# Row maxima of attention scores by a relu and an add-max, in an attention-and-scan kernel

## The chip, the core and the metric

The kernel runs on one core of a Trainium2 chip. The metric is the device time of one launch in microseconds (us). The core has a matrix engine (TensorE, PE in the views; its weight loads are PEld), a vector engine (VectorE, DVE), an activation engine (ScalarE, ACT), GpSimd (POOL) and SyncE (SP), which issues the DMAs. Each engine runs its own queue in order and waits on semaphores for the others.

## The reference

For 16 images of 256 channels by 32 x 32 pixels (1024 tokens) two residual layers are computed in f32. Only the first layer's attention is touched here:

```
tok  = gn(x) + pos
qkv  = layernorm(tok) @ w_qkv                  # 4 heads of 32
dots = einsum('bihd,bjhd->bhij', q, k) * 32**-0.5
attn = softmax(dots, axis=-1)                  # 1024 x 1024 per head
out  = einsum('bhij,bjhd->bihd', attn, v)
tok  = out @ w_out + b_out + tok               # then a feed-forward part
```

The second layer is a state-space model: convolutions and projections, then a scan over the 1024 tokens, h = dA * h + (d_t * u_t) * B_t, for 512 channels x 64 states, an output y = sum of h * C_t, a gate and a projection.

The softmax subtracts the largest score of each row. The kernel needs these row maxima before it can compute exp(dots - max).

## The kernel before, in words

**The scan sets the pace.** For every image there are 256 scan units (`UNITS`), each of 128 partitions x 1024 tokens. A unit is a DMA of one broadcast row block (`load`, tile `dub`), a multiplication on GpSimd (`inputs`, L905), a matmul with 48 rows for the decay (`decay`, L914) and its exp on ScalarE (L916), both in a two-bank PSUM tile `a` with two buffers, and `tensor_tensor_scan` on VectorE (`scan`, L922). After eight units the 64 states are summed on TensorE (`outputs`, L947 and L959, tile `yb`), with copies out by ScalarE (L953, L963).

**All other work is fitted in between.** The layers around the scan are Python generators. Image b+1's attention and scan inputs, and image b-1's gate, run beside image b's scan: the main loop (from L1000) calls, per unit, in this order: load, inputs, the next pieces of `outputs`, scan of unit n, decay of unit n+2, and then one piece of the side work, up to its next `yield`. At the end of the build every compute engine's instructions are tied to the order in which they were written (L1048 to L1058), so that each queue holds exactly this interleaving. Only the first image's attention runs with no scan beside it.

**PSUM has eight banks.** Four belong to the decays (`aps`), one to `yb`, one to accumulations (`accp`), and two to everything else (`mm`). `psum()` takes from `mm` while the scan runs; before the scan it also takes the banks of `aps` in turn.

**The maxima stage** (L411 to L448 of `attention_layer`). `q4` and `k4` hold the queries and keys of the four heads, 32 partitions each, 1024 tokens wide. The loop has 32 steps: 16 chunks of 64 queries (c) x 2 halves of 512 keys (hf). A step begins with `maxima()`, which lets VectorE reduce the two tiles that the step before wrote (L416, tensor_reduce max, PSUM 128x512 to one column of `mx`). Then two PSUM tiles are taken, one for each pair of heads g, and four matmuls (L435), one per head, fill them: 64 queries of each head on 64 partitions, 512 keys wide. Each step also issues one of the DMAs that bring the heads into the layout of the next stage (`to_space`). Then it yields, and the main loop goes on with a scan unit. After the loop the two halves are joined and negated by one more reduce (L445), and TensorE turns the result (L447) for use as a further row of the queries.

After that come the values, the scores again in the other orientation with exp on ScalarE (L503, L511), and the rest of the layer. The tiles of L511 come from the pool `ptp` (tag "pt", four buffers).

Of the kernel before, what the change touches and what calls it, by code (L numbers as in the profile page):

```python
# [11 lines left out]
F32 = mybir.dt.float32  # L12
BF16 = mybir.dt.bfloat16
AF = mybir.ActivationFunctionType
ALU = mybir.AluOpType
AX = mybir.AxisListType
# [3 lines left out]
P = 128  # L20
# [3 lines left out]
HL = 512  # L24
NG = 16
HEADS, DH = 4, 32
INNER = HEADS * DH
NJ = L // P
# [22 lines left out]
def attention_then_scan_kernel(  # L51
# [18 lines left out]
    nc = tc.nc  # L70
    B = x.shape[0]

    def pool(name, bufs, **kw):
        return ctx.enter_context(tc.tile_pool(name=name, bufs=bufs, **kw))
# [5 lines left out]
    ptp = pool("ptp", 4)  # L80
    small = pool("small", 2)
# [14 lines left out]
    def bank(src, name):  # L96
        return src.tile([P, HL], F32, name=name, tag="mm" if src is mm else "av")

    def free_bank(name):
        if spare:  # L100
            return spare.pop()
        if next(alone) is mm:
            return bank(mm, name)
        both = aps.tile([P, L], F32, name=name, tag="a")
        spare.append(both[:, hs(1)])
        return both[:, hs(0)]

    def psum(name, dims=P):
        return (bank(mm, name) if beside["scan"] else free_bank(name))[:dims]
# [7 lines left out]
    def work(name, n=L):  # L117
        return wide.tile([P, L + 2 + CONV], F32, name=name, tag="wide")[:, :n]

    def hwork(name):  # L120
        return half.tile([P, HL], F32, name=name, tag="half")

    def hs(h):
        return ts(h, HL)
# [37 lines left out]
    for k in range(ND):  # L162
# [4 lines left out]
        for j in range(2):  # L167
# [3 lines left out]
                start=(j == 0), stop=(j == 1),  # L171
# [32 lines left out]
    t = work("ones_s")[:1]  # L204
# [3 lines left out]
    for k in range(KC):  # L208
        t = work("rel_s").rearrange("p (i j) -> p i j", j=32)
# [156 lines left out]
    def attention_layer(b):  # L366
# [23 lines left out]
        q4, k4 = work("q4"), work("k4")  # L390
# [17 lines left out]

        mx = small.tile([P, 2, 2 * NJ, 2], F32, name="mx", tag="mx")  # L411
        waiting = []

        def maxima():
            for s, g, c, hf in waiting:
                nc.vector.tensor_reduce(mx[:, g, c, hf : hf + 1], s, AX.X, ALU.max)  # L416
            waiting.clear()

        def against(pair, e):
# [3 lines left out]
        to_space = [  # L423
            partial(spaced, to, src, pair)
            for pair in range(HEADS // 2) for to, src in ((qas, q4), (kas, k4))
        ] + [partial(against, pair, e) for pair in range(HEADS // 2) for e in range(2)]
        for c in range(2 * NJ):
            for hf in range(2):
                maxima()
                for g in range(2):  # L430
                    waiting.append((psum("s_ps"), g, c, hf))
                for h in range(HEADS):
                    g, e = divmod(h, 2)
                    r = ts(h, DH)
                    nc.tensor.matmul(  # L435
                        waiting[g][0][ts(e, 64)], q4[r, ts(c, 64)], k4[r, hs(hf)],
                        start=True, stop=True,
                    )
                if to_space:
                    to_space.pop(0)()  # L440
                yield 1
        maxima()
        del q4, k4, to_space
        neg = small.tile([P, HEADS * NJ], F32, name="neg", tag="neg")
        nc.vector.tensor_reduce(neg, mx.rearrange("p g c k -> p (g c) k"), AX.X, ALU.max, negate=True)  # L445
        ps = psum("neg_ps", HEADS * NJ)[:, :P]
        nc.tensor.matmul(ps, neg, ident, start=True, stop=True)  # L447
        yield 1  # L448
# [2 lines left out]
        for h in range(HEADS):  # L451
            pair, e = divmod(h, 2)
# [6 lines left out]
        for g in range(2):  # L459
            t = work("vv").rearrange("p (j h e) -> p j h e", j=NJ // 2, h=HEADS)  # L460
            nc.vector.memset(t[:, :, :, DH:], 1.0)
            ps = psum("v_ps").rearrange("p (j e) -> p j e", j=NJ // 2)
            for j in range(NJ // 2):
                for k in range(KC):
                    nc.tensor.matmul(
                        ps[:, j, :], xn[k][:, ts(g * (NJ // 2) + j, P)], wv_s[:, k, :],
                        start=(k == 0), stop=(k == KC - 1),
# [14 lines left out]
        for pair in range(HEADS // 2):  # L482
# [3 lines left out]
            for hf in range(2):  # L486
# [11 lines left out]
                for j in range(NJ):  # L498
                    scores = []
                    for e in range(2):  # L500
                        r = ds(2 * DH * e, DH + 1)
                        s = psum("st_ps")
# [6 lines left out]
                    for s in scores:  # L509
                        pt = ptp.tile([P, HL], F32, name="pt", tag="pt")  # L510
# [35 lines left out]
        for hf in range(2):  # L546
            nc.vector.tensor_tensor(ao[:, hs(hf)], ao[:, hs(hf)], sums[:, hs(hf)], ALU.mult)
            for k in range(KC):
                for i, ps in outs:
                    if i == k:  # L550
                        t = tok[k][:, hs(0)]
# [7 lines left out]
        for k, ps in outs:  # L559
            t = tok[k][:, hs(1)]  # L560
# [22 lines left out]
        for hf in range(3):  # L583
            for k, ps in enumerate(outs):
                t = xs[k][:, hs(hf - 1)]
# [386 lines left out]
    def prepare(b):  # L972
        return chain(first_norm(b), attention_layer(b), scan_inputs(b))
# [26 lines left out]
    for n, (b, k, q, e, i) in enumerate(units):  # L1000
        at = n % UNITS
        if at == 0:
            parts = [prepare(b + 1)] if b + 1 < B else []
            total = steps * len(parts)
            if b > 0:
                parts = [first_norm(b + 1), gate_and_store(b - 1), attention_layer(b + 1), scan_inputs(b + 1)]
                if b + 1 == B:
                    parts = parts[1:2]
                total = total + GATE
            side = chain(*parts)  # L1010
            rate, due = rate_for(total, UNITS - AHEAD - 3), 0.0
# [102 lines left out]
```

## Time and profile before

| | |
|---|---|
| median of 3 runs | 13106.57 us (13067.61 to 13129.75) |
| profiled execution, its own time | 13096.86 us |
| its span, first to last instruction | 13095.1 us |
| mean granted TensorE clock | 0.800 |
| L922 scan, VectorE | 4096 x 2278 ns, 9215.1 us |
| L905 multiplication, GpSimd | 4096 x 2417 ns, 9810.6 us |
| L916 exp of the decay, ScalarE | 4096 x 1090 ns, 4462.8 us |
| L416 reduces of the maxima, VectorE | 1023 x 681 ns, 649.0 us in this row |
| L435 matmuls of the maxima, TensorE | 4092 records, mean 619 ns as the row has it |

The page of a profile gives each engine's busy time and its share of the span, then groups of instructions: line, engine, operation, output <- input by the program's names, shapes, count; then busy time, mean length of one in ns, and the idle time of the engine just ahead of them with what ended it. The timeline view gives start and length in us and merges neighbours of one group ("x2"). An f32 matmul appears as two records, each with its own weight load. Records of one engine may overlap a little, as each counts its way through the pipeline. An idle time in square brackets is that of the engine before the instruction. A windows view gives the busy time of each engine in a stretch.

### The profile page before, as it was taken

To read this page: it belongs to the slowest core of one execution; us is meant where nothing else is said; L and a number is where in the kernel's file an instruction comes from. 1 tells how busy PE (TensorE), PEld (TensorE's weight loads), DVE (VectorE), ACT (ScalarE), POOL (GpSimd) and SP (SyncE) were. 2 spreads that over 40 slices of the span, in tenths; PEclk is the share of its full clock that TensorE was granted. 3 is DMA by queue.
4 is the path that set the end of the run, shared out by engine and by line. 5 is a ranking of instruction groups with operands and counts; after the bars stand their busy time and mean duration, and the time that the engine had idled before them with its cause. 6 is when DMAs were issued, how large, how long until landed. Compare 5 with 4: busy or idle time off the path is not lost.

```text
span 13095.1 us, 424083 instructions
## 1 busy us (share of the span) xinstructions
PE 9717.3 (74%) x186800; PEld 5456.0 (42%) x186800; DVE 11666.7 (89%) x7560; ACT 7520.3 (57%) x10421; POOL 9815.4 (75%) x4105
## 2 busy tenths in 40 slices
PE   6676876868778687786868767687686877868767
PEld 2344443444444344443444434444344444444445
DVE  3789999899999899988999898999989899889998
ACT  2465664655646556565665656566465664655654
POOL 0487876878778787786877768787687877878798
PEclk8887977879788697887879878797787977869755
DMA  1467666676666767666666666766667666676676
GB/s 52 165 220 238 208 218 218 220 243 201 221 216 219 235 200 233 216 220 231 211 224 218 213 223 213 236 210 219 218 218 234 205 218 217 218 236 204 227 248 231
DMA packets 1038401, 2820.10 MB, mean 215 GB/s; under 512 B 290370, under 2 KB 368451, under 8 KB 1036548
## 3 DMA queue, kind: packets, MB, share of 16 engines
q1 hardware_dynamic: 1036548, 2792.97, 64.6%
q8 instruction: 1459, 23.90, 0.7%
q14 instruction: 394, 3.23, 0.1%
HBM read 2513.82 MB, written 261.62 MB: 212 GB/s over the span
## 4 chain that ended last, share of the span: by engine, by line
DVE 36%; PE 31%; issue 13%; ACT 11%; DMA 6%; POOL 2%; SPq 1%; DVEq 0%; POOLq 0%; ACTq 0%
DVE h L922 25%; PE yb L947 6%; ACT a L916 5%; DVE mx L416 5%; PE a L914 5%; PE av L491 3%; PE g_ps L688 2%; DMA dub<-dus 2%; PE st_ps L503 2%; POOL dub L905 2%; PE z_ps L639 2%; PE yb L959 1%; PE m_ps L859 1%; PE qk_ps L403 1%; DVE u L674 1%
## 5 line engine op out<-in xcount | busy, mean ns | idle before, releaser
L905 POOL TENSOR_TENSOR dub<-dub,bt 128x1024 f32<-128x1024 f32 x4096 | 9810.6, 2417 | 3229.8 <-DMA dub<-dus 2896.6
L922 DVE TENSOR_TENSOR_SCAN h<-a,dub 128x1024 f32<-128x1024 f32 x4096 | 9215.1, 2278 | 752.0 <-ACT a L916 401.8
L916 ACT ACTIVATE a<-a,acol 128x1024 f32<-128x1024 f32 x4096 | 4462.8, 1090 | 3253.4 <-PE a L914 3206.7
L914 PE MATMUL a<-pieces,pick 48*128 48x512 bf16 x8192 | 1902.6, 455 | 2518.2 <-DVE h L922 2401.8
L947 PEld LDWEIGHTS yb<-h,cd 128*32 128x32 f32 x131072 | 2488.2, 128 | 2781.3 <-issue 1265.6
L947 PE MATMUL yb<-h,cd 128*32 128x64 f32 x131072 | 3255.8, 252 | 476.8 <-ACT y L953 325.2
L914 PEld LDWEIGHTS <-pick 48*128 48x128 bf16 x8192 | 603.3, 95 | 2915.4 <-issue 2467.5
L953 ACT COPY y<-yb 128x256 f32<-128x256 f32 x2048 | 763.6, 373 | 914.7 <-PE yb L947 907.5
L435 PE MATMUL s_ps<-k,q 32*64 32x512 f32 x4092 | 825.7, 619 | 95.5 <-DVE mx L416 95.0
L416 DVE TENSOR_REDUCE mx<-s_ps 128x1 f32<-128x512 f32 x1023 | 649.0, 681 | 15.5 <-PE s_ps L435 15.5
L491 PE MATMUL av<-pt,vv 128*64 128x512 f32 x2048 | 596.1, 662 | 3.0 <-ACT sums L480 1.7
L959 PE MATMUL yb<-turn,y 128*32 128x16 f32 x32768 | 591.4, 214 | 5.8 <-issue 4.9
L511 ACT ACTIVATE pt<-st_ps 128x512 f32<-128x512 f32 x1024 | 554.1, 599 | 60.9 <-PE st_ps L503 59.9
L959 PEld LDWEIGHTS yb<-turn,y 128*32 128x32 f32 x32768 | 573.8, 159 | 6.6 <-issue 5.2
L503 PE MATMUL st_ps<-sp 33*128 33x512 f32 x2048 | 561.8, 622 | 4.5 <-ACT pt L511 3.3
L963 ACT COPY yo<-yb 128x128 f32<-128x128 f32 x512 | 136.1, 266 | 587.8 <-PE yb L959 560.5
L688 PE MATMUL g_ps<-w,xp 128*128 128x256 f32 x1464 | 451.9, 447 | 0.0
L688 PEld LDWEIGHTS g_ps<-w,xp 128*128 128x128 f32 x1464 | 367.3, 326 | 65.5 <-issue 54.0
L435 PEld LDWEIGHTS s_ps<-k,q 32*64 32x64 f32 x4092 | 193.6, 131 | 440.8 <-DVE mx L416 421.1
L859 PE MATMUL m_ps<-w,xs 128*128 128x256 f32 x1024 | 317.5, 460 | 10.4 <-DVE xs L834 10.4
L674 DVE SCALAR_TENSOR_TENSOR u<-up,cwh,u 128x1024 f32<-128x1024 f32 x192 | 273.0, 1422 | 28.0 <-ACT u L666 27.7
L859 PEld LDWEIGHTS m_ps<-w,xs 128*128 128x128 f32 x1024 | 262.1, 328 | 55.9 <-issue 32.0
(177 smaller groups left out, 6690.8 us busy)
## 6 DMA issues: line engine op xcount, KB each, us to landing
dub<-dus SPq DMA_DIRECT2D x4096, 512.0 KB
dps<-pc SPq DMA_DIRECT2D x384, 128.0 KB
pieces<-dps SPq DMA_DIRECT2D x1024, 48.0 KB
xs<-in_x_dram SPq DMA_DIRECT2D x64, 512.0 KB
xs<-kept SPq DMA_DIRECT2D x64, 512.0 KB
zs<-z SPq DMA_DIRECT2D x64, 512.0 KB
ud<-u SPq DMA_DIRECT2D x64, 512.0 KB
dus<-du SPq DMA_DIRECT2D x64, 512.0 KB
```

What stands on the lines that cost most here:

```text
L416: nc.vector.tensor_reduce(mx[:, g, c, hf : hf + 1], s, AX.X, ALU.max)
L435: nc.tensor.matmul(waiting[g][0][ts(e, 64)], q4[r, ts(c, 64)], k4[r, hs(hf)], start=True, stop=True,)
L491: nc.tensor.matmul(av[ts(e, 2 * DH)], vv[j // (NJ // 2)][:, j % (NJ // 2), 2 * pair + e, :], pts[e], start=(j == 0), stop=(j == NJ - 1),)
L503: nc.tensor.matmul(s, ka[r, ts(j, P)], qa[r, hs(hf)], start=True, stop=True)
L688: nc.tensor.matmul(ps[:, ts(q, C)], xp[k][:, ds(first + t, P, 4)], wg_s[:, k, t, :], start=(k == 0 and t == 0), stop=False,)
L905: nc.gpsimd.tensor_tensor(v, v, blocks[units[n][0]]["bt"], ALU.mult)
L914: nc.tensor.matmul(a[:, hs(hf)], w, pieces[r], start=True, stop=True)
L916: nc.scalar.activation(a, a, AF.Exp, scale=acol[:, at : at + 1])
L922: nc.vector.tensor_tensor_scan(now["h", e][:, i, :], decays.pop(n), loaded.pop(n), 0.0, ALU.mult, ALU.add)
L947: nc.tensor.matmul(yb[ts(g, 32), ts(s, 64)], cd[:, at // 16, ts(c, 32)], hbuf[:, :, at : at + 8], start=(c == 0), stop=(c == 1),)
L953: nc.scalar.copy(y2[:, r], yb[:, :256])
L959: nc.tensor.matmul(some[ts(r, 32), x], y2[:, r, x:256:8], turn[:, x], start=True, stop=True)
```

## The change

The two halves of the keys are no longer treated alike. With s = q . k_hi (the second half of the keys) and d = q . (k_lo - k_hi), the larger of the two halves' scores is s + relu(d), key by key. So:

- one subtraction on VectorE makes `kd`, the difference of the key halves, once per image;
- a step now handles one pair of heads g and one chunk of queries: two tiles, s against the second half of the keys and d against `kd`, each filled by two matmuls, of the same two heads;
- ScalarE writes relu(d) into an SBUF tile `over` (from `ptp`) one step later;
- VectorE, two steps after the matmuls, adds s and `over` and takes the maximum along the row, in one `tensor_tensor_reduce`, written in the built program as two instructions (the operation and a read of the accumulator into a column of `mx`);
- `mx` has 32 columns in place of 64, and the joining reduce becomes a multiplication by -1;
- after the loop `maxima()` is called twice, to empty both lists.

There are as many steps, matmuls and DMAs as before: 32 steps, four matmuls in each. The lines behind the change stand nine lower in the changed kernel (L922 becomes L931, for example).

```diff
-        mx = small.tile([P, 2, 2 * NJ, 2], F32, name="mx", tag="mx")
-        waiting = []
+        mx = small.tile([P, 2 * 2 * NJ], F32, name="mx", tag="mx")
+        kd = hwork("kd")
+        nc.vector.tensor_tensor(kd, k4[:, hs(0)], k4[:, hs(1)], ALU.subtract)
+        waiting, above = [], []
 
         def maxima():
-            for s, g, c, hf in waiting:
-                nc.vector.tensor_reduce(mx[:, g, c, hf : hf + 1], s, AX.X, ALU.max)
+            for s, r, at in above:
+                nc.vector.tensor_tensor_reduce(
+                    r, s, r, 1.0, -3.0e38, ALU.add, ALU.max, mx[:, at : at + 1]
+                )
+            above.clear()
+            for s, d, at in waiting:
+                r = ptp.tile([P, HL], F32, name="over", tag="pt")
+                nc.scalar.activation(r, d, AF.Relu)
+                above.append((s, r, at))
             waiting.clear()
...
         for c in range(2 * NJ):
-            for hf in range(2):
+            for g in range(2):
                 maxima()
-                for g in range(2):
-                    waiting.append((psum("s_ps"), g, c, hf))
-                for h in range(HEADS):
-                    g, e = divmod(h, 2)
-                    r = ts(h, DH)
-                    nc.tensor.matmul(
-                        waiting[g][0][ts(e, 64)], q4[r, ts(c, 64)], k4[r, hs(hf)],
-                        start=True, stop=True,
-                    )
+                pair = [psum("s_ps") for _ in range(2)]
+                for t, keys in zip(pair, (k4[:, hs(1)], kd)):
+                    for e in range(2):
+                        r = ts(2 * g + e, DH)
+                        nc.tensor.matmul(
+                            t[ts(e, 64)], q4[r, ts(c, 64)], keys[r], start=True, stop=True
+                        )
+                waiting.append((*pair, g * 2 * NJ + c))
                 if to_space:
                     to_space.pop(0)()
                 yield 1
         maxima()
-        del q4, k4, to_space
+        maxima()
+        del q4, k4, to_space, kd, pair, t, keys
         neg = small.tile([P, HEADS * NJ], F32, name="neg", tag="neg")
-        nc.vector.tensor_reduce(neg, mx.rearrange("p g c k -> p (g c) k"), AX.X, ALU.max, negate=True)
+        nc.vector.tensor_scalar(neg, mx, -1.0, None, ALU.mult)
```

## The prediction

> **What bounds the kernel now.** I read the engine totals first, then the costliest groups, then the stretch in which the changed lines run, then one step of that stretch on the timeline.
>
> ```profile
> PE 9717.3 (74%) x186800; PEld 5456.0 (42%) x186800; DVE 11666.7 (89%) x7560; ACT 7520.3 (57%) x10421; POOL 9815.4 (75%) x4105
> ...
> L416 DVE TENSOR_REDUCE mx<-s_ps 128x1 f32<-128x512 f32 x1023 | 649.0, 681 | 15.5 <-PE s_ps L435 15.5
> ```
>
> VectorE is the busiest engine, and the maxima are some 650 us of it; they wait only 15.5 us for their scores. The windows view of one batch's maxima stretch, the second that runs beside the scan (length, then busy time of PE, PEld, DVE, ACT, POOL; granted clock; DMA share; GB/s):
>
> ```profile
> 1376.00:1486.00 110.00, 88.19 (x1647) 38.46 (x1636) 109.47 (x99) 43.80 (x55) 78.56 (x34) 1.00 0.55 175
> ```
>
> VectorE is busy for 109.47 of 110 us, at full TensorE clock. This stretch is bound by VectorE alone. One step of it on the timeline (start, length, engine, line):
>
> ```profile
> 1382.36 1.26 DVE L416 TENSOR_REDUCE mx<-s_ps 128x1 f32<-128x512 f32 x2
> ...
> 1382.50 0.39 PE L914 MATMUL a<-pieces,pick 48*128 48x512 bf16 x2 [0.54 <-DVE h L922]
> ...
> 1382.93 1.09 ACT L916 ACTIVATE a<-a,acol 128x1024 f32<-128x1024 f32 x1 [0.53 <-PE a L914]
> 1383.08 0.19 PEld L435 LDWEIGHTS s_ps<-k,q 32*64 32x64 f32 x4 [0.49 <-DVE mx L416]
> ...
> 1383.54 2.28 DVE L922 TENSOR_TENSOR_SCAN h<-a,dub 128x1024 f32<-128x1024 f32 x1
> ...
> 1384.68 0.49 PEld L947 LDWEIGHTS yb<-h,cd 128*32 128x32 f32 x32 [0.81 <-ACT a L916]
> 1384.68 0.65 PE L947 MATMUL yb<-h,cd 128*32 128x64 f32 x32
> 1385.27 0.09 PEld L914 LDWEIGHTS <-pick 48*128 48x128 bf16 x1
> ...
> 1385.73 1.27 DVE L416 TENSOR_REDUCE mx<-s_ps 128x1 f32<-128x512 f32 x2
> ```
>
> A step lasts 3.37 us (1382.36 to 1385.73; 3.377 in all 15 batches that run beside the scan): two reduces, 1.18 from start to the scan's start, and one scan, 2.20 until the next reduce. Everything else has room: the decay's exp (1382.93 to 1384.02) is for the scan after the one that starts at 1383.54.
>
> **The intended part.** In place of two reduces (0.58 us each, start to start) VectorE gets one add-max and a read of its accumulator (the built program shows two instructions for one call). The add-max reads a PSUM and an SBUF tile and writes SBUF. Its row is missing; below it lies 0.67 us (L310, same operands), above it 1.25 us (L547, two SBUF inputs):
>
> ```profile
> L310 DVE TENSOR_TENSOR xn<-xs,ln_m 128x512 f32<-128x512 f32 x126 | 79.6, 673 | 13.5 <-PE ln_m L303 13.1
> ...
> L547 DVE TENSOR_TENSOR ao<-ao,sums 128x512 f32<-128x512 f32 x32 | 39.8, 1246 | 66.5 <-DMA sums<-den 47.7 <-DMA dub<-dus 18.8
> ```
>
> I take 0.67, being nearest. The accumulator read costs between nothing and 0.22 us (L445, a reduce to 32 columns). VectorE's own sum would be 2.20 + 0.58 to 0.67 + 0 to 0.22: about 2.8 to 3.1 us a step, against 3.377.
>
> **The wait that takes its place.** Beside the scan the pool of score banks has two banks. Before, both are freed by VectorE in one go. Now a step's two tiles s (half the keys) and d (the difference) are freed by two engines: d by the relu on ScalarE one step later, s by the add-max two steps later. In the built program the scores s of step n wait for ScalarE, d of step n waits for VectorE. The queues are fixed: TensorE has s(n), d(n), the output matmuls (L947), the next decay (L914), then s(n+1); ScalarE has the decay's exp (L916) and behind it relu(n). So relu(n-1) lets s(n) go, and everything up to relu(n) follows in series. Who waits: behind s(n) on TensorE stands the decay, behind that exp, behind exp the relu, and the add-max on VectorE holds the following scan. One turn of this ring, each link from a row:
>
> ```profile
> 1376.65 1.09 PE L435 MATMUL s_ps<-k,q 32*64 32x512 f32 x8
> ...
> 1377.67 0.49 PEld L947 LDWEIGHTS yb<-h,cd 128*32 128x32 f32 x32 [0.81 <-ACT y L953]
> ...
> 1391.43 0.49 PEld L947 LDWEIGHTS yb<-h,cd 128*32 128x32 f32 x32 [0.81 <-ACT a L916]
> ...
> 1392.98 0.10 PEld L914 LDWEIGHTS <-pick 48*128 48x128 bf16 x2
> ...
> 1393.42 1.09 ACT L916 ACTIVATE a<-a,acol 128x1024 f32<-128x1024 f32 x1
> ```
>
> - Relu's end to s's weight load: 0.05 us, as from a ScalarE copy to TensorE (1328.02 to 1328.07).
> - s and d: before, four heads on four row groups, 1.02 us until the next weight load (1376.65 to 1377.67). Now s and d of one step use the same two heads, so the same row groups, and follow each other: two more passes at 0.43 each (the f32 passes of L303 start at 1336.00 and 1336.43): 1.88. The add-max lies beside: 0.10 + 0.67 + 0.05 = 0.82, before s's two passes (0.91) are through. Without that cover, at 1.25 us, it adds some 0.45.
> - Output matmuls, 1384.68 to 1385.27: 0.59. In one step of eight the turn (L959) comes in as well, 1391.43 to 1392.98: 0.96 more, 0.12 on average.
> - Decay's load to exp's start: 0.44 (1392.98 to 1393.42).
> - Exp's start to the next activation's start: 1.00 (L916 at 1512.29, L511 at 1513.30).
> - Relu: 0.60, from L511 (599 ns, PSUM to SBUF, same shape); L665 (587) and L765 (657, a relu in place in PSUM) bound it. No table load: the relu of L765 has none beside the exps, and the built program has as many loads as before.
>
> Sum: 0.05 + 1.88 + 0.59 + 0.12 + 0.44 + 1.00 + 0.60 = 4.68 us a step, against 3.377: **+1.30 us**. VectorE then idles some 1.6 us per step.
>
> By the rows it makes little difference which engine takes a relu: at 128x512 f32 an activation took 599 ns and a VectorE operation 673. The Trainium skill, page "ScalarE: Activation LUTs", section "Rules for kernel authors", speaks against the place: it puts relu on VectorE, and budgets 0.3 us plus 0.83 ns per element for an activation. By that budget a relu would be an estimated 0.73 us and the whole forecast some 60 us higher; the rows do not bear it out, and I stay with them.
>
> **The sum.** In each of 15 batches 31 steps lie between first and last maximum: 15 x 31 x 1.30 = 605 us. The last add-max follows another without a scan between, so one scan a batch is no longer hidden in the ring: 15 x 2.2 = 33. The subtraction that makes kd stands in VectorE's queue ahead of a scan: 0.67 to 1.25 (same rows), 15 x 1.25 = 19, as it has two SBUF inputs like L547. The final negation is a small operation for a small reduce: nothing. The first batch's maxima run before any scan and with more banks: 54.6 us from first to last reduce, and TensorE would need 32 x 4 x 0.43 = 55: between -5 and +7, I take +2. The DMA issues are the same ones in the same steps; SP's queue only spreads. The relu's tiles come from the pool of four that the exps of L511 use only afterwards. ScalarE's 512 relus (307 us) and TensorE's longer occupation lie in the ring and are in its sum. Together +659 us on the profiled execution's 13,096.9: **13,756 us**, +5%. The median of the runs is 9.7 us above that execution, less than their spread, so I forecast the same for it.
>
> **Rivals.**
> 1. *VectorE stays the bound, faster.* If the ring were shorter than VectorE's work, a step would take 2.8 to 3.1 us: 465 x (-0.58 to -0.28) = -270 to -130, plus 21: about 12,900. For it speaks VectorE's 109.47 of 110. Against it: with two banks, the ring needs a third of its links gone (4.68 to 3.1).
> 2. *The add-max is slow.* At 1.25 us it, not s, holds d back: +0.45 x 465 = +209, so 13,965. For it: two instructions instead of one, nothing like it in the trace.
> 3. *The ring is looser.* Some links overlap (s and d partly in parallel, 0.43 to 0.86 less): 3.8 to 4.25 a step, 13,350 to 13,560. For it: heads on different row groups do overlap in the trace (1376.65). Against it: here the groups are the same. Decides from the point at which half a link goes.
> 4. *Nothing measurable*: the ring happens to be near 3.3 us; no link suggests it.
>
> **How the numbers follow.** Chances: forecast (13,560 to 13,860) 0.62; rival 2 (13,860 to 14,100) 0.18; rival 3 0.10; rival 1 0.06; rival 4 0.04. Rivals 1, 4 and most of 3 are left out (2 in 10); the range takes in the add-max's upper bound: 13,530 to 13,990. Half a per cent is 65 us, about what a measurement of this kernel can tell from no change: faster 0.06, same 0.04, slower 0.90.
>
> **What would show it.** In the profile after: a step of about 4.7 us between add-maxes (5.6 with the turn), VectorE idle 1.5 us in each, put down to the relu; scores s waiting for ScalarE; the windows view of a maxima stretch at some 150 us with VectorE at two thirds. Add-max rows near 0.67 us confirm that link, rows near 1.25 rival 2. If steps are near 3 us and VectorE is full, the ring doesn't bind and I am wrong altogether.

## The result, and the profile after

The changed kernel takes 14849.2 us (median, 14833.98 to 14886.51), the kernel before 13093.9 in the same comparison: ratio 1.134, 95% interval 1.131 to 1.137. The profiled execution spans 14847.6 us against 13095.1, 1752.5 more. The forecast was 13,756, with 13,990 as the upper end: the direction was right, the loss 2.7 times as large as forecast.

The page of the changed kernel, totals and the groups of the change (its lines stand nine lower than before from the scan on):

```profile
PE 10981.1 (74%) x186800; PEld 5771.4 (39%) x186800; DVE 11433.5 (77%) x7576; ACT 7783.9 (52%) x10933; POOL 9816.9 (66%) x4105
...
L418 DVE CUSTOM_DVE_ANT_0 over<-s_ps,over 128x512 f32<-128x512 f32 x511 | 351.1, 689 | 1761.6 <-ACT over L424 1761.4
...
L443 PE MATMUL s_ps<-k,q 32*64 32x512 f32 x2044 | 961.2, 1055 | 796.7 <-ACT over L424 796.7
L443 PE MATMUL s_ps<-kd,q 32*64 32x512 f32 x2048 | 939.4, 1031 | 12.9 <-DVE kd L413 7.2 <-DVE mx L418 5.8
...
L424 ACT ACTIVATE over<-s_ps 128x512 f32<-128x512 f32 x512 | 300.6, 589 | 51.3 <-PE s_ps L443 51.2
```

VectorE does less than before (11433.5 us for 11666.7) and now waits 1761 us for the relu ahead of its add-maxes. The add-max takes 0.69 us, as hoped. The records of the score matmuls (two to a matmul) take 1.03 to 1.06 us each; before they took 0.62. The windows view of one maxima stretch, the second beside the scan (columns as before: length; busy PE, PEld, DVE, ACT, POOL; granted clock; DMA share; GB/s):

```profile
1516.00:1736.00 220.00, 165.93 (x1558) 57.10 (x1558) 88.55 (x96) 57.11 (x83) 77.22 (x33) 0.50 0.24 82
```

The stretch is twice as long, VectorE is busy for 40% of it, and **the granted clock is 0.50, where it was 1.00 before**. One step on the timeline:

```profile
1601.54 0.29 PEld L443 LDWEIGHTS s_ps<-k,q 32*64 32x64 f32 x4 [2.20 <-ACT over L424]
...
1605.14 0.84 PEld L956 LDWEIGHTS yb<-h,cd 128*32 128x32 f32 x32 [1.61 <-issue]
...
1606.16 0.11 PEld L923 LDWEIGHTS <-pick 48*128 48x128 bf16 x2 [0.17 <-issue]
...
1606.81 1.09 ACT L925 ACTIVATE a<-a,acol 128x1024 f32<-128x1024 f32 x1
1607.82 0.59 ACT L424 ACTIVATE over<-s_ps 128x512 f32<-128x512 f32 x1
...
1608.46 0.29 PEld L443 LDWEIGHTS s_ps<-k,q 32*64 32x64 f32 x4 [2.20 <-ACT over L424]
```

This is the predicted ring, link by link: scores 3.60 us, output matmuls 1.02, decay to exp 0.65, exp 1.01, relu 0.59 and 0.05 to the next scores: 6.92 us. The links on TensorE are near double what was taken (1.88, 0.59, 0.44); those on ScalarE are as taken. All 15 stretches beside the scan have this step (6.93 us; 7.74 with the turn), last 217.0 to 218.6 us from the start of the first add-max to that of the last, against 105.26 for the reduces, and sit at half clock from at most 6 us after their first score matmul, but for 3.4 us in two of them. That is 1697 of the 1752.5 us; the first batch's stretch adds 12.2 (66.9 for 54.7).

### The profile page after: what moved, and what is told of

Read it like the earlier page. It is cut to its first block, busy times and chain, and to the rows that moved or that the text cites. A ratio compares the mean times of both kernels' runs of the same rounds, so it can differ in the third digit from the quotient of the medians.

```text
span 14847.6 us, 425573 instructions
## 1 busy us (share of the span) xinstructions
PE 10981.1 (74%) x186800; PEld 5771.4 (39%) x186800; DVE 11433.5 (77%) x7576; ACT 7783.9 (52%) x10933; POOL 9816.9 (66%) x4105
## 4 chain that ended last, share of the span: by engine, by line
PE 44%; DVE 24%; ACT 13%; issue 10%; DMA 5%; POOL 2%; SPq 1%; DVEq 0%; POOLq 0%; ACTq 0%
DVE h L931 18%; PE s_ps L443 12%; PE yb L956 8%; ACT a L925 6%; PE a L923 6%; PE av L500 3%; PE g_ps L697 2%; DMA dub<-dus 2%; PE st_ps L512 2%; ACT over L424 2%; PE yb L968 2%; PE z_ps L648 2%; POOL dub L914 2%; PE m_ps L868 1%; PE qk_ps L403 1%
## 5 line engine op out<-in xcount | busy, mean ns | idle before, releaser
L914 POOL TENSOR_TENSOR dub<-dub,bt 128x1024 f32<-128x1024 f32 x4096 | 9812.1, 2424 | 4980.9 <-DMA dub<-dus 4752.1
L931 DVE TENSOR_TENSOR_SCAN h<-a,dub 128x1024 f32<-128x1024 f32 x4096 | 9214.8, 2278 | 998.4 <-PE yb L956 402.2
L956 PEld LDWEIGHTS yb<-h,cd 128*32 128x32 f32 x131072 | 2658.8, 135 | 3174.8 <-issue 1895.5
L956 PE MATMUL yb<-h,cd 128*32 128x64 f32 x131072 | 3464.4, 263 | 487.6 <-ACT y L962 327.5
L923 PE MATMUL a<-pieces,pick 48*128 48x512 bf16 x8192 | 2007.0, 481 | 2262.4 <-DVE h L931 2149.0
L418 DVE CUSTOM_DVE_ANT_0 over<-s_ps,over 128x512 f32<-128x512 f32 x511 | 351.1, 689 | 1761.6 <-ACT over L424 1761.4
L923 PEld LDWEIGHTS <-pick 48*128 48x128 bf16 x8192 | 571.0, 96 | 2700.7 <-issue 2290.2
L443 PE MATMUL s_ps<-k,q 32*64 32x512 f32 x2044 | 961.2, 1055 | 796.7 <-ACT over L424 796.7
L443 PE MATMUL s_ps<-kd,q 32*64 32x512 f32 x2048 | 939.4, 1031 | 12.9 <-DVE kd L413 7.2
L443 PEld LDWEIGHTS s_ps<-k,q 32*64 32x64 f32 x2044 | 144.8, 198 | 1052.1 <-ACT over L424 1038.8
L443 PEld LDWEIGHTS s_ps<-kd,q 32*64 32x64 f32 x2048 | 226.6, 220 | 622.7 <-DVE mx L418 303.3
L697 PEld LDWEIGHTS g_ps<-w,xp 128*128 128x128 f32 x1464 | 367.1, 326 | 65.6 <-issue 54.7
L424 ACT ACTIVATE over<-s_ps 128x512 f32<-128x512 f32 x512 | 300.6, 589 | 51.3 <-PE s_ps L443 51.2
```

The lines of the kernel that those rows point to most:

```text
L424: nc.scalar.activation(r, d, AF.Relu)
L443: nc.tensor.matmul(t[ts(e, 64)], q4[r, ts(c, 64)], keys[r], start=True, stop=True)
L697: nc.tensor.matmul(ps[:, ts(q, C)], xp[k][:, ds(first + t, P, 4)], wg_s[:, k, t, :], start=(k == 0 and t == 0), stop=False,)
L914: nc.gpsimd.tensor_tensor(v, v, blocks[units[n][0]]["bt"], ALU.mult)
L923: nc.tensor.matmul(a[:, hs(hf)], w, pieces[r], start=True, stop=True)
L931: nc.vector.tensor_tensor_scan(now["h", e][:, i, :], decays.pop(n), loaded.pop(n), 0.0, ALU.mult, ALU.add)
```

## The experiments

That the ring binds was the forecast; its size was not. So the first question is what halved the clock: **theory A**, TensorE's waiting in the ring; **theory B**, the kind of matmul (two row groups of the array in place of four); **theory C**, neither. The second is whether cutting the ring gives the time back. Some of the kernels add matmuls whose results nobody reads. The first edit is against the kernel before, that of the small filling against the kernel with the filled gap, the others against the changed kernel; "..." stands for lines left out.

**One pair of heads per step, in the kernel before.**

```diff
-            for hf in range(2):
+            for g in range(2):
                 maxima()
-                for g in range(2):
+                for hf in range(2):
                     waiting.append((psum("s_ps"), g, c, hf))
-                for h in range(HEADS):
-                    g, e = divmod(h, 2)
...
+                for hf in range(2):
+                    for e in range(2):
+                        r = ts(2 * g + e, DH)
...
```

> One part of the change alone: the kernel before, but a step fills its two tiles for one pair of heads and both halves of the keys (as the changed kernel orders them), not for both pairs and one half. Both tiles are still reduced by VectorE. Theory A (TensorE's clock is halved because the new ring of waits leaves TensorE idle for part of every step): no ring here, VectorE stays the bound, a step 3.38 us, granted clock about 1.0 in the maxima stretches, total within 0.5% of the kernel before. Theory B (the clock is halved by the kind of matmul: two row groups busy at a time in place of four): clock 0.5 in the maxima stretches; at the half-clock durations of the changed kernel (3.60 us for the two tiles, 1.02 for the output matmuls, 0.65 for the decay) TensorE alone needs 5.3 us a step, total about 13,990.

Measured: 13084.97 us, ratio 0.9999 (0.998 to 1.002). A step is 3.377 us as before, the clock 1.00 in every stretch. A stretch in the windows view:

```profile
1382.00:1487.00 105.00, 93.70 (x1590) 39.27 (x1591) 105.00 (x94) 40.04 (x51) 74.93 (x32) 1.00 0.53 176
```

Theory B is out: this kind of matmul alone costs nothing while VectorE sets the pace.

**The gap filled.**

```diff
+        warm = accp.tile([P, HL], F32, name="warm", tag="av")
...
                 maxima()
+                for _ in range(2):
+                    nc.tensor.matmul(warm, ident, q4[:, hs(0)], start=True, stop=True)
...
```

> The changed kernel with two more f32 matmuls (128x128 weights, 512 columns, 0.86 us each at full clock) ahead of each step's scores, into a PSUM tile that nobody reads; they fit into the 1.6 to 2.2 us in which TensorE waits for the relu. Theory A: the clock returns to about 1.0 in the maxima stretches and the ring comes down to the predicted 4.7 us a step: 13,094 + 605 for the ring + 52 for the scan and the subtraction + some 70 for the first batch, where the added matmuls aren't hidden: about 13,820, faster than the changed kernel though it does more. Theory C (the half clock is not due to the idle time): the added matmuls take 3.4 us at half clock, 1.2 more than the gap, and the total rises to about 15,400.

Measured: 13869.27 us, ratio 1.060 (1.058 to 1.062): 980 us less than the changed kernel, with more work. A step on the timeline of this kernel:

```profile
1560.74 1.98 PE L441 MATMUL warm<-q,ident 128*128 128x512 f32 x4
1560.88 1.09 ACT L928 ACTIVATE a<-a,acol 128x1024 f32<-128x1024 f32 x1 [3.11 <-PE a L926]
...
1561.89 0.59 ACT L425 ACTIVATE over<-s_ps 128x512 f32<-128x512 f32 x1
...
1562.66 1.07 PE L446 MATMUL s_ps<-k,q 32*64 32x512 f32 x4
...
1564.52 0.49 PEld L959 LDWEIGHTS yb<-h,cd 128*32 128x32 f32 x32 [0.81 <-issue]
...
1565.10 0.10 PEld L926 LDWEIGHTS <-pick 48*128 48x128 bf16 x2
```

The clock is 1.00, and scores to output matmuls take 1.86 us, output matmuls 0.58: the ring as forecast (its steps 4.71 us in the median, against 4.68 forecast on average; here the added matmuls themselves hold the scores back by some 0.15). Theory C is out. The half clock is a consequence of what TensorE did, not a disturbance, and the ring without it costs what was predicted.

**The relu at once.**

```diff
...
-            for s, d, at in waiting:
-                r = ptp.tile([P, HL], F32, name="over", tag="pt")
-                nc.scalar.activation(r, d, AF.Relu)
-                above.append((s, r, at))
-            waiting.clear()
...
-                waiting.append((*pair, g * 2 * NJ + c))
+                over = ptp.tile([P, HL], F32, name="over", tag="pt")
+                nc.scalar.activation(over, pair[1], AF.Relu)
+                above.append((pair[0], over, g * 2 * NJ + c))
...
```

> The changed kernel with the relu written right behind the matmuls of its own step, and the add-max one step later instead of two. The relu then stands ahead of the next decay's exp on ScalarE, and the ring through decay and exp is cut: the score bank of the next step is free when its relu ends, about 1 us after the second tile. If the ring is the cause of the loss: VectorE bounds the step again, scan 2.20 + add-max 0.61 + accumulator read, 2.85 to 3.0 us, TensorE busy for 2.9 of it and at full clock, total 13,094 - 465 x 0.45 + 20 = about 12,900 (12,850 to 12,990), faster than the kernel before. If the extra engine hop costs by itself, wherever the relu stands: still over 13,300.

Measured: 13281.31 us (median of four, 13163 to 13418); ratio 1.012 (1.006 to 1.018) by the three up to 13316. A miss, and the most telling run. Two of its stretches in the windows view:

```profile
1376.00:1540.00 164.00, 163.81 (x1570) 57.14 (x1563) 90.41 (x94) 59.07 (x82) 76.14 (x33) 0.50 0.33 113
2234.00:2329.00 95.00, 91.12 (x1560) 38.20 (x1559) 89.36 (x97) 58.75 (x83) 73.36 (x32) 1.00 0.56 190
```

The same instructions take 164 us in one stretch and 95 in another. At full clock the step is 3.06 us, shorter than before (3.377): without the ring through decay and exp the change does save time. At half clock it is 5.16 us and TensorE itself is the bound, busy for 163.81 of 164 us. All 15 stretches have full clock when their first score matmul starts. Six stay there; the other nine drop to half within 5 us, two for good, the rest for 20 us or more. So theory A in its plain form, that the clock follows the share of time in which TensorE is busy, can't be right: here TensorE has a record running all the time, and the clock doesn't come back.

**A third bank.**

```diff
-                pair = [psum("s_ps") for _ in range(2)]
+                pair = [psum("s_ps"), bank(accp, "d_ps") if beside["scan"] else psum("s_ps")]
```

> The changed kernel with a third score bank beside the scan: d goes into the accumulation bank (not in use at that time), s alternates between the two others. s no longer waits for the relu; the ring has only d, output matmuls, decay, exp and relu. At full clock 0.05 + 1.02 + 0.59 + 0.44 + 1.00 + 0.59 + 0.12 = 3.8 us a step, total about 13,350; at half clock (1.9 for d, 1.02, 0.65, 1.01, 0.59, 0.15) 5.4 us, total about 14,090. TensorE would be busy for 75% of a step at full clock (61% in the changed kernel's ring, 81% before, which had full clock): which of the two clocks it gets tells where the limit lies. If two banks are not what closes the ring, the time stays at 14,850.

Measured: 13953.87 us, ratio 1.066 (1.063 to 1.069): the half-clock case, with a step of 5.22 us against 5.4 expected. Taking s out of the ring shortens it by 1.7 us, so two banks were what closed it through s. The clock falls here too, though nine of the 15 stretches return to 1.0 for 3 to 20 us at a time. In the pieces at full clock a plain step is 3.68 us.

**A version faster than both.** The relu at once, the third bank, and s of one pair of heads beside d of the other, so that four row groups work side by side as before the change:

```diff
...
+                maxima(1 if g == 0 else 0)
+                pair = [psum("s_ps"), bank(accp, "d_ps") if beside["scan"] else psum("s_ps")]
+                for e in range(2):
+                    for t, keys, p in zip(pair, (k4[:, hs(1)], kd), (g, 1 - g)):
+                        r = ts(2 * p + e, DH)
+                        nc.tensor.matmul(
+                            t[ts(e, 64)], q4[r, ts(c, 64)], keys[r], start=True, stop=True
+                        )
+                over = ptp.tile([P, HL], F32, name="over", tag="pt")
+                nc.scalar.activation(over, pair[1], AF.Relu)
+                late["s", g], late["r", 1 - g] = pair[0], over
+                if g == 1:
+                    for p in range(2):
+                        above.append((late["s", p], late["r", p], p * 2 * NJ + c))
...
```

> A version meant to be faster than both: relu right behind its matmuls, d in the accumulation bank beside the scan, and a step takes s of one pair of heads and d of the other pair, so that four row groups work side by side (1.07 us in place of 1.88). At full clock TensorE needs 2.1 us a step, VectorE 2.20 + 0.60 + 0.08 = 2.88, which bounds it: 13,095 + 15 x (31 x 2.88 + 1 - 105.3) + 15 x 1.8 for the subtraction = about 12,900. Theory D (the clock follows the work that the matmul array gets done per us, not the share of time in which TensorE is busy, since the relu-at-once kernel sat at half clock while busy for 99.9% of the stretch): one step's work per 2.88 us is more than before (3.38 us, full clock), so full clock where it enters with it; at half clock a step takes 3.6 us, and the total is at most 13,240. Theory A (busy share alone): 72% busy at full clock, less than the 81% of before and the 75% at which the changed kernel sat at half clock: it falls to half clock in all stretches, 13,240.

Measured: 12868.67 us, ratio 0.984 (0.981 to 0.987): 1.6% less than the kernel before, a small gain, but clear of the noise. Its step and a stretch (timeline, then windows view):

```profile
1420.19 0.08 DVE L419 DVE_READ_ACCUMULATOR2_ANT mx<- 128x1 f32 x1
1420.19 2.28 DVE L931 TENSOR_TENSOR_SCAN h<-a,dub 128x1024 f32<-128x1024 f32 x1
...
1421.48 0.60 ACT L442 ACTIVATE over<-d_ps 128x512 f32<-128x512 f32 x1 [0.23 <-PE d_ps L438]
...
1422.40 0.67 DVE L419 CUSTOM_DVE_ANT_0 over<-s_ps,over 128x512 f32<-128x512 f32 x1
...
1422.98 2.28 DVE L931 TENSOR_TENSOR_SCAN h<-a,dub 128x1024 f32<-128x1024 f32 x1
```

```profile
1375.00:1460.00 85.00, 65.27 (x1518) 30.22 (x1516) 84.97 (x94) 57.66 (x81) 70.15 (x31) 1.00 0.63 203
```

VectorE bounds the stretch again, with scan and add-max back to back: 2.79 us a step, 84.4 us from the first add-max to the last. TensorE is busy for 77% of it and yet at full clock, where theory A expected half; but it had taken 72%, and the kernel before was at 80%, so this alone says little against the busy share. In 11 of the 15 stretches the clock drops to half some 2 us after the first score matmul, as in the relu-at-once kernel, but here it is back after 3.4 to 6.8 us.

**Small filling.** The next runs ask what the clock does follow. **Theory D**: the multiplications that the matmul array gets done per us.

```diff
-                for _ in range(2):
-                    nc.tensor.matmul(warm, ident, q4[:, hs(0)], start=True, stop=True)
+                for _ in range(2):
+                    for e in range(2):
+                        r = ts(e, DH)
+                        nc.tensor.matmul(
+                            warm[ts(e, 64)], q4[r, ts(c, 64)], k4[r, hs(0)], start=True, stop=True
+                        )
```

> As the kernel with the filled gap, but the added matmuls are as small as the scores' own (two heads, 32 rows by 64 columns each): the same TensorE time per step (1.7 us at full clock), a quarter of the array. Theory A (busy share alone decides the clock): full clock, about 13,870 as with the large ones. Theory D (work of the array per us): the clock stays at 0.5, the added matmuls take 3.5 us against a gap of 2.2, a step 8.2 us, total about 15,500.

Measured: 13766.79 us, ratio 1.052 (1.049 to 1.055), full clock in all stretches, and a step of 4.56 us, 5.35 with the turn: the plain ring. One stretch:

```profile
1452.00:1598.00 146.00, 143.93 (x1800) 50.56 (x1798) 88.19 (x94) 55.48 (x83) 77.26 (x33) 1.00 0.37 124
```

That is theory A's number, but the expectation for D was badly derived: it took for granted that a stretch starts at half clock. Every stretch starts at full clock, and at 4.56 us a step this kernel does 6.9 million multiplications per us, no less than the kernel before (6.8). So the run decides nothing between A and D.

**Wide and short, narrow and long.** One added matmul of 128x128 weights and 256 columns; or two of a single head, 32x64 weights and 512 columns, one behind the other.

```diff
...
+                nc.tensor.matmul(warm[:, :256], ident, q4[:, :256], start=True, stop=True)
...
```

> The changed kernel with one added matmul per step that is short but uses the whole array: 128x128 weights, 256 f32 columns, 0.43 us at full clock, result not read. Counted as multiplications (rows x columns of weights x moving columns, per record), a step has 8.4 million for the scores, 8.4 for the output matmuls and 6.3 for the decay, 23.1 in all; the added one has 8.4. Theory D (the clock is kept while the array gets enough multiplications done per us; the limit lies between 6.1, the third-bank kernel at full clock, which fell, and 6.8, the kernel before, which stayed): 31.5 per 4.56 us is 6.9, so full clock, a step 4.56 us (5.35 with the turn), total about 13,770. Theory A (share of time in which TensorE is busy): (2.86 + 0.43) / 4.56 = 72%, less than the 75% at which the third-bank kernel fell: half clock, a step 6.93 us, total about 14,860.

```diff
...
+                for _ in range(2):
+                    nc.tensor.matmul(
+                        warm[:64], q4[:DH, ts(c, 64)], k4[:DH, hs(0)], start=True, stop=True
+                    )
...
```

> The opposite: two added matmuls per step of one head each time (32 rows by 64 columns, 512 f32 columns), one behind the other: 1.72 us at full clock, so TensorE is as long busy as in the two kernels with the filled gap, but only 4.2 million multiplications. Theory D: 27.3 per 4.56 us is 6.0, below the limit: half clock, the added matmuls take 3.5 us against a gap of 2.2, a step about 8.2 us, total about 15,400. Theory A: 98% busy, full clock, a step 4.56 us, total about 13,770.

Measured: 14725.21 us (1.125, 1.122 to 1.129) and 15217.09 (1.165, 1.162 to 1.167). Both at half clock from at most 15 us after the first score matmul, the first with short returns in most stretches. The second one's step is 7.05 us in the median, 7.68 on average, against 8.2 expected. A stretch of each in the windows view:

```profile
1500.00:1709.00 209.00, 187.86 (x1618) 68.84 (x1618) 88.44 (x94) 56.66 (x83) 76.66 (x33) 0.55 0.26 87
```

```profile
1610.00:1848.00 238.00, 236.29 (x1680) 78.53 (x1678) 88.06 (x94) 56.98 (x83) 77.33 (x33) 0.51 0.23 76
```

The narrow one is busy for 236.29 of 238 us and gets half the clock: A is out. The wide one falls with as many multiplications as the small filling, which stayed: D is out. What both have alike is the rows of the array times the columns that stream through them, 508 thousand a step: **theory E**.

**One wide matmul, and the same with a quarter of the weights.**

```diff
...
+                nc.tensor.matmul(warm, ident, q4[:, hs(0)], start=True, stop=True)
...
```

> The changed kernel with one added f32 matmul per step, 128x128 weights, 512 columns (0.86 us at full clock), result not read. Theory E: the clock is kept by what streams through the array, counted as rows of the array in use x moving columns per record, without regard to the weight columns. A step has 8 x 32 x 512 for the scores, 32 x 128 x 64 for the output matmuls and 2 x 48 x 512 for the decay: 442 thousand. Per us of the step at full clock: before 131 (stayed full), small filling 126 (stayed full), third bank 116 (fell), wide-short and narrow-long filling 111 (fell), changed kernel 97 (fell). Here 573 / 4.56 = 126: full clock, a step 4.56 us, total about 13,780. Theory D (multiplications) expects the same, 39.9 / 4.56 = 8.7. Theory A (busy share): (2.86 + 0.86) / 4.56 = 82%; it has no clear answer any more, since 98% fell in the narrow-long kernel and 85% stayed in the pair-per-step kernel.

```diff
...
+                nc.tensor.matmul(warm[:32], ident[:, :32], q4[:, hs(0)], start=True, stop=True)
...
```

> As the one before, but with 128x32 weights: the same rows and the same moving columns, a quarter of the multiplications. Theory E: 126 again, full clock, a step 4.56 us, total about 13,780. Theory D: (23.1 + 4.2) / 4.56 = 6.0 million per us, the same as in the narrow-long kernel, which fell: half clock, a step 6.93 us, total about 14,860.

Measured: 13782.26 us (1.055, 1.052 to 1.057) and 13778.70 (1.054, 1.051 to 1.057), both with the step of 4.56 us. The second one's windows view:

```profile
1470.00:1610.00 140.00, 116.11 (x1565) 39.44 (x1565) 84.29 (x90) 53.01 (x79) 71.74 (x31) 0.99 0.34 115
```

With the narrow-long kernel's multiplications (6.0 million per us) and less busy time than it, it has full clock (0.99 in this window, whose last 2.5 us lie behind the stretch). E forecast it, D didn't. Worked out for all kernels (thousand rows x columns of a step's records, divided by the step's length at full clock):

| kernel | per step | step, us | per us | clock in the stretches |
|---|---|---|---|---|
| faster version | 442 | 2.79 | 158 | 1.0, but for some openings |
| gap filled | 704 | 4.71 | 149 | 1.0 |
| before; pair per step | 442 | 3.377 | 131 | 1.0 |
| small filling; wide one; rows only | 573 | 4.56 | 126 | 1.0 |
| third bank | 442 | 3.68 | 120 | 0.5, in part 1.0 |
| wide short; narrow long | 508 | 4.56 | 111 | 0.5, the first in part 1.0 |
| changed kernel | 442 | 4.56 | 97 | 0.5 |

So in these stretches the limit, by this count, lies between 120 and 126 thousand rows x columns per us. Three things qualify it.

First, the openings. The relu-at-once kernel does 144 at its full-clock step of 3.06 us, and yet nine of its stretches fall as they open, like eleven of the faster version (158). There the first d waits for the subtraction (1.9 us on average in both); that this wait makes them fall is argued, not tried. Once at half clock, the relu-at-once kernel does 86 thousand per us (a step of 5.16 us) and is caught; the faster version comes back.

Second, 262 of the 442 thousand are the output matmuls. The experiments vary only the added matmuls, so they don't fix what the common work counts: with any figure from some 190 to 550 thousand for it (worked out from the steps in the table) the kernels come in an order that fits, with another limit.

Third, the count is no rule for the rest of the program. Near the end of the kernel before, with no side work left on TensorE:

```profile
13001.00:13052.00 51.00, 39.70 (x1019) 27.70 (x1021) 48.03 (x22) 26.63 (x35) 44.76 (x20) 0.50 0.68 215
```

These are output matmuls (787 records of L947, 192 of L959) and decays (40 of L914), 153 thousand rows x columns per us, and the clock is at half. So what the chip's monitor counts isn't shown; of the three counts tried (busy share, multiplications, rows x columns) the last is the one that fits the maxima stretches of all twelve kernels, openings aside.

## Why the prediction was wrong, point by point

- *What bounds the kernel.* Right: VectorE alone, shown by the pair-per-step kernel, where longer matmuls changed nothing.
- *The intended part.* Right: the add-max took 0.69 us (0.67 taken), the accumulator read 0.08. Scan plus add-max come to 2.79 us where nothing else binds, at the low end of the 2.8 to 3.1 forecast.
- *The wait that takes its place.* Right: VectorE waits for the relu, the scores for the relu too, for the reason given. With the relu at once the step is 3.06 us at full clock, with a third bank 3.68.
- *The links of the ring.* The sum was right at full clock: 4.56 us in a plain step by its terms without the turn, 4.56 measured in three kernels with added matmuls (the turn adds 0.79, with 0.96 taken). **The step that failed is that every TensorE link was priced from rows at full clock**, because the stretch had full clock before. The change took away what kept it: TensorE's work per step stayed the same and the step grew longer, so the work per us fell under the limit (from 131 to 97 thousand by the count above), the clock was halved, and the step grew further. The TensorE links 1.88 + 0.59 + 0.44 = 2.91 became 3.60 + 1.02 + 0.65 = 5.27; 2.36 us more in 465 steps is 1097 us, and the miss was 1093; the other terms together were right to a few us (54 taken, 56 measured).
- *Could it have been seen?* The page gave a mean granted clock of 0.800, so half clock was common outside this stretch, and the prediction read "at full TensorE clock" off the windows view without asking what it hangs on. No rival held a slower clock, and the upper end of the range, set by the add-max, bounded the wrong term.
- *The relu and the tables.* Right: 589 ns (0.60 taken), no load beside it.
- *The subtraction.* Taken at 1.25 us; it took 1.83 on average (0.67 to 2.41). *The first batch*: +2 taken, +12.2 measured, also at a lower clock (0.77 in its stretch for 0.88). For the subtraction and the scan no longer hidden 52 us were taken; outside the stretches 43 are left over. That the two misses nearly cancel is luck.
- *Rivals.* None came about. Rival 1, VectorE as the bound, is what the faster version does, at 12,869 for the 12,900 named there; but not in this change.

The Trainium skill's page "TensorE: Matmul & The Clock Gate", section "What's actually happening", has a gate that knows two rates and decides by windows of 3413 ns; the trace agrees, with granted clocks of 0.5 and 1.0 only, in pieces that are multiples of 3.41 us, but for the last one of a run. The same page's section "HAM oscillation — how this bites in real kernels" gives the rule that TensorE must have no idle gaps over some 3.4 us. The runs differ: the changed kernel's gaps were 1.7 us and it had half clock nearly throughout, and two kernels had it while busy for over 99% of a stretch.

## What to carry to other kernels

When two buffers that one engine freed are freed by two engines in turn, follow the queues from each release to the next: if a relu waits behind an exp that waits behind a matmul that waits for the buffer, the step is the sum of all of them, not the work of the busiest engine. Any forecast that lengthens a step must then ask whether TensorE still does enough per us to keep its clock, and price the TensorE links at both clocks. Writing the consumer of a tile right behind its producer, and keeping all row groups of the array in use, with a third bank, turned this change from 13% slower to 1.6% faster.

## What the runs showed of the hardware that was not expected

- TensorE's clock can be halved while its records are without a gap: 163.81 of 164 us busy at clock 0.50. What the added matmuls are decides: 1.72 us a step (by full clock) of single-head ones (32 rows) left the clock at 0.51; the same time of two heads at once (13,767 us) or 0.86 us of one with 128 rows (13,782 us) held it at 1.00.
- A stretch can have two lengths: 95 and 164 us with the same instructions, by whether the clock falls as it opens. The caught stretches of the relu-at-once kernel that got free did so some 25, 70, 111 or 153 us after their first score matmul, about one round of eight steps apart (8 x 5.16 + 0.9 = 42 us); each round holds one turn. That the turn frees them is argued, not tried.
- More work made a kernel faster by 7%: the filled gap (13,869 us for 14,849).
